# An adaLN transformer block: the last feed-forward's residual and modulation on other engines, another order for the first projections, new planner costs

## The chip, the cores and the metric

The kernel runs on one core of a Trainium2 chip. The metric is the device time of one execution in microseconds (us), lower is better. TensorE (PE) multiplies matrices and transposes, VectorE (DVE) does elementwise work and reductions, ScalarE (ACT) does activations and copies, GpSimd (POOL) does elementwise work that stays in SBUF, and SyncE (SP) issues nearly all DMAs.

## The reference

Two sequences (b = 0, 1) of 2048 tokens with 256 features go through one block:

```
mod = (silu(c) @ wmod)            # six rows of 256 per sequence: sa, ca, ga, sb, cb, gb
ga, gb = sign(.) * max(|.|, 0.25)
h = layernorm(x) * (1 + ca) + sa
q, k, v = h @ wq, h @ wk, h @ wv  # 16 heads, key size 16, value size 64
p = softmax(q k^T / 4, over the queries)      # axis=1: each key normalises over all queries
x = x + ga * ((p @ v) @ wo)
h = layernorm(x) * (1 + cb) + sb
x = x + gb * fp4_linear(silu(fp4_linear(h, w_gate)) * fp4_linear(h, w_up), w_down)
```

`fp4_linear` rounds both operands in blocks of 16 to the grid 0, 0.5, 1, 1.5, 2, 3, 4, 6 times (block maximum / 6). The hidden size is 704. All is float32.

## The kernel before, in words

A planner, not the program's text, sets the order of instructions. Every piece of work is a generator (a *chain*) that yields operations, waits for events and for rooms (buffers), and is added with a due time counted in attention steps. `Order.run` simulates the engines: each operation has a cost from `Queue.estimate` (L285), a dependent one waits for its forerunner (`SAME` on one engine, 0.2 us between engines), and on each engine the operation that can start first goes first, ties by due time. `Free(op)` drops the tie to the chain's previous operation. `Best(first, second, margin)` picks the first engine unless the second would end more than `margin` earlier. The result is a fixed list for each engine; the engines then run their lists strictly in order and wait on semaphores.

The work, in order of time:

- **The start.** The four groups of 512 tokens of x, `wm_a` (sa and ca), wq, wk and `wm_b` (the other modulation rows) are loaded. `mod_columns` (L476) makes silu(c), multiplies it with `wm_a` on TensorE (tile `modt`, 16 small matmuls), and brings the two results out of PSUM on DVE as `sa_t` and `ca1_t`. `norm(0, g)` takes layer-norm statistics on DVE, applies them (`xn`), transposes with TensorE and modulates the transposed tokens (`ht`). `qk(0, 0, i, g)` projects the first eight heads' queries (i = 0) and keys (i = 1) of one group, splits the result into two parts (`st`), and sends it by SP both into the first head's tiles (`q<-st`, two DMAs; `k<-st`, four) and to a DRAM scratch. The first attention step waits for all four query groups and for the first key group. `mod_rows` makes the remaining modulation rows (`modb`, then `mods`).
- **The middle.** 512 attention steps (2 sequences, 16 heads, 16 key tiles): scores on TensorE (`ps`), a pass with a minimum on DVE (`e`), `mn` on POOL, exp on ACT, the reciprocal `rz` on DVE, scaled values `vn` on POOL, and the product with the values on TensorE (`o`). Between the steps lie the projections, the rounding of the weights, and the whole feed-forward of sequence 0.
- **The tail.** Sequence 1's feed-forward has nothing left to hide behind. `project_last` adds the last quad of heads into x (`op` on TensorE, the sum on DVE). `ffn_stats` takes statistics for 1, 3 or 4 tiles of 128 tokens, `tail_norm` applies them (`ffn_apply`: one scale-and-shift, then times `cb` and plus `sb` from `mods`) and rounds with `quantize` (tiles `w`, `am_h`, `s_h`, `r_h`), and `tail(b, t)` does for each of 16 tiles: transpose (`hq`), gate and up projections (`pg`, `pu`), silu and product, `quantize` again (`e`, `am_g`, `s_g`, `r_g`), transpose (`h2t`), down projection (`dn`, weights already times gb), sum with x (`y`) and the store. Tile 15 is cut into two halves (`tail_part`).

`quantize` finds the block maximum `am`, the scale `s = am / 6` with an exact correction (three more small operations), its reciprocal `r`, and then runs five wide passes; the choice between POOL and DVE or ACT and DVE is by margin (`QUANTIZE_MARGIN`, `TAIL_MARGIN`).

Of the kernel before, what the change touches and what calls it, by code (L numbers as in the profile page):

```python
# [32 lines left out]
NPACE = 0.2  # L33
FPACE = 0.4
FFN = 9
MODS_DUE = 3, 4.0
WEIGHTS_DUE = 6, 210
COPY_MARGIN = 0.5
QUANTIZE_MARGIN = 2
WEIGHTS_MARGIN = 3  # L40
TAIL_MARGIN = 1


PROJECT_DUE = -0.5, 1.2, 2, 2
NORM_DUE = -0.4, -0.2, 0.6
STATS_LEAD = 4
NORM_LEAD = 2.5
LAST_LEAD = 0.5
SPLIT = 1
MODS = ("ga", "sb", "cb", "gb")  # L50
# [190 lines left out]
class Queue:  # L241
# [23 lines left out]
    def estimate(self, method, args, kw, emit):  # L265
        out = args[0]
        aps = [a for a in args if isinstance(a, bass.AP)]
        n = max(size(a) for a in aps)
        if method == "dma_start":
            return 0.5, emit, 2.3 + n * out.shape[0] * 4e-6 / 0.35  # L270
        if self.name == "PE":
            if method == "transpose":
                return out.shape[0] / 1200, emit, 0.0, None, "full"

            lhsT, rhs = kw["lhsT"], kw["rhs"]
            passes = 1 if rhs.dtype == F32R else 2
            stream = size(rhs) * passes ** 2 / 2400
            if rhs.shape[0] <= 64:
                first = lhsT.start_partition() == 0
                return (stream + 0.002 if first else 0.005), emit, 0.0, None, "rows"  # L280
            if out.shape[0] <= 64:
                first = out.start_partition() == 0
                return (stream + 0.005 if first else 0.005), emit, 0.0, None, "columns"
            return stream + 0.005, emit, 0.0, None, "full"
        sb = all(a.space != PSUM for a in aps)  # L285
        if self.name == "ACT":
            t = 0.05 + n / 1200 + 0.04 * sb
            func = kw.get("func", args[2] if method == "activation" else None)
            table = {AF.Exp: "exp", AF.Silu: "silu"}.get(func)
            t += 0.093 * sum(isinstance(kw.get(k), bass.AP) for k in ("bias", "scale"))  # L290
            t += 0.17 * isinstance(kw.get("accum_out"), bass.AP)
            return t, emit, 0.0, table
        if self.name == "POOL":
            if method == "tensor_scalar":
                return 0.16 + 0.083 * len(aps[2:]) + n * 0.001, emit
            if n == 1:
                return 0.28, emit
            spread = any(len(a.ap) > 2 and a.ap[-1][0] == 0 for a in aps)
            return 0.08 + n * (0.0019 if spread else 0.0023), emit
        if method == "reciprocal":  # L300
            return 0.07 + n * 0.0063, emit
        scalars = method == "tensor_scalar" and len(aps) > 2
        fast = method in ("tensor_scalar", "tensor_copy") and sb and not scalars
        if fast:
            return 0.065 + n * 0.00052, emit
        if "accum_out" in kw:
            return 0.065 + 0.07 * scalars + n * 0.00104, emit, 0.05
        return 0.03 + 0.035 * (not sb) + 0.06 * (scalars and not sb) + n * 0.00104, emit


@with_exitstack
def adaln_block(
# [85 lines left out]
    def copy(dst, src, margin=None):  # L398
        return either(A.copy(dst, src), V.tensor_copy(dst, src), margin)

    def matmuls(dst, pairs):
        return [
            T.matmul(dst, lhsT=l, rhs=r, start=(k == 0), stop=(k == len(pairs) - 1))
            for k, (l, r) in enumerate(pairs)
        ]

# [65 lines left out]
    nc.gpsimd.memset(magic[:, 0:1], 1.5 * 2.0 ** 22)  # L472
    nc.gpsimd.memset(magic[:, 1:2], -1.5 * 2.0 ** 22)


    def mod_columns():  # L476

        yield Wait(["c"])
        yield A.activation(sig, cs, AF.Exp, scale=-1.0)
        yield V.tensor_scalar(sig, sig, 1.0, None, ALU.add)  # L480
        yield V.reciprocal(sig, sig)
        yield V.tensor_tensor(cs, cs, sig, ALU.mult)
        signal("cs")
        place, _ = yield Wait(["wm_a"], OTHER)
        ps = banks(place, "modt")[:, 0, 0 : 2 * KC * B].rearrange("p (j b) -> p j b", b=B)
        for j in range(2 * KC):
            yield Free(
                matmuls(
                    ps[:, j, :],
                    [(wm_a[:, k, j * P : (j + 1) * P], cs[:, k, :]) for k in range(KC)],  # L490
                )
            )
        give("osb")
        yield V.tensor_copy(sa_t, ps[:, 0:KC, :])
        yield V.tensor_scalar(ca1_t, ps[:, KC :, :], 1.0, None, ALU.add)
        leave(place)
        signal("sa")

# [40 lines left out]
        signal("mods")  # L539


    def ln_stats(x4, name):

        n = x4.shape[1]
        yield Wait(take=["ln"])
# [19 lines left out]
                yield V.scalar_tensor_tensor(r, e, 1.5, r, ALU.add, ALU.mult)  # L565
        yield V.scalar_tensor_tensor(e, e, 0.5, r, ALU.add, ALU.mult)
        yield V.tensor_tensor(r, r, e, ALU.add)
        yield V.scalar_tensor_tensor(c, mv[:, 0:n, 0], -1.0, r, ALU.mult, ALU.mult)
        return c, r

# [13 lines left out]
    SIXTH = 1.0 / 6.0  # L584

    EXPONENT = 0x7F800000

    def blocks(a):
        return a.rearrange("p (n k) -> p n k", k=BLK)
# [20 lines left out]
    def quantize(a, nb, name, m, margin=None):  # L610

        a3 = blocks(a)
        s, r = yield from scales(a3, nb, name)
        yield V.tensor_scalar(r, r, 1.0 - 2.0 ** -23, None, ALU.mult)  # L620
        yield pool(a3, a3, spread(r), ALU.mult, margin=QUANTIZE_MARGIN if margin is None else None)
        yield V.tensor_scalar(m.bitcast(U32), a.bitcast(U32), EXPONENT, None, ALU.bitwise_and)
        yield either(

            [
                A.activation(m, m, AF.Relu, bias=magic[:, 1:2], scale=1.5 * 2.0 ** 22),
                A.activation(m, m, AF.Identity, bias=magic[:, 0:1]),
            ],
            V.tensor_scalar(m, m, 1.0, 1.5 * 2.0 ** 22, ALU.max, ALU.mult),
            margin,  # L630
        )
# [223 lines left out]

    def qk(b, blk, i, n):

        room = "v" if (b, blk, i) == (0, 0, 1) else "st"
        place, _, _ = yield Wait([("ht", b, n), "wk" if i else "wq"], [*OTHER, room])
        if (b, i, blk) not in scratch:  # L860
            scratch[b, i, blk] = dram.tile(
# [290 lines left out]
    def ffn_stats(b, t, n):  # L1152
        yield Wait([("out", b, NQUAD - 1, t + j) for j in range(n)])
        x4 = xs[b, t // 4][:, t % 4 : t % 4 + n, :]
        c, r = yield from ln_stats(x4, f"f{b}_{t}")
        for j in range(n):
            lns[b, t + j] = (c, r, j, n)
        signal(("ln", b, t))

    def ffn_apply(h, b, t, margin=None):  # L1160
        c, r, j, n = lns[b, t]
        yield ln_apply(h, x_tile(b, t), j, c, r, margin)
        if signal(("applied", b, t - j), of=n):
            give("ln")
        for which, op in (("cb", ALU.mult), ("sb", ALU.add)):
            args = h, h, mod(b, which), op
            op = G.tensor_tensor(*args)
            yield op if margin is None else Best(op, V.tensor_tensor(*args), margin=margin)

    def finish(ps, y, place, b, t):  # L1170
        yield V.tensor_tensor(y, ps[:, 0:D], mod(b, "gb"), ALU.mult)
# [79 lines left out]
            )  # L1251
        signal("wdb")

    def down(ps, h2t, wd):
        return matmuls(ps[:, 0:D], down_pairs(h2t, wd))
# [17 lines left out]
    def tail(b, t):  # L1273
# [46 lines left out]
        yield from transpose_hidden(e, h2t, f"h2t{b}_{t}", TAIL_MARGIN)  # L1320
        yield Wait(["wdb"], ["o"])
        ps = ps_o.tile([P, 512], F32, tag="o", name=f"dn{b}_{t}")
        for c, op in enumerate(down(ps, h2t, tails["w"])):
            yield Free(op) if c else op
        give("e")
        yield from tail_out(b, t, ps)

    def tail_out(b, t, ps):
        yield Wait(take=["h"])
        y = w2.tile([P, D], F32, tag="h", name=f"y{b}_{t}")  # L1330
        yield V.tensor_tensor(y, ps[:, 0:D], x_tile(b, t), ALU.add)
        give("o")
        yield S.dma_start(out[b, t * P : (t + 1) * P, :], y)
        give("h")
# [1 line left out]
    def tail_part(b, t, i, e, pg, pu, places):  # L1336
# [17 lines left out]
        if i == 0:  # L1354
            yield Wait(["wdb"], ["o"])
            tails["o", b, t] = ps_o.tile([P, 512], F32, tag="o", name=f"dn{b}_{t}")
        else:
            yield Wait([("down", b, t)])
        ps = tails["o", b, t]
        for c, r in enumerate(CHUNK[3 * i : 3 * i + 3]):  # L1360
# [4 lines left out]
                start=(i == 0 and c == 0),  # L1365
                stop=(i == 1 and c == 2),
            )
        signal(("down", b, t))
# [126 lines left out]
```

## Time and profile before

| | |
|---|---|
| median of 3 runs | 2009.36 us (2007.64 to 2009.44) |
| profiled execution: its own time | 2009.48 us |
| its span, first to last instruction | 2007.4 us |
| busy: PE, DVE, ACT, POOL | 1913.4, 1728.3, 1328.1, 696.5 us |
| first score matmul, last attention matmul ends | 46.95 us, about 1806.1 us |
| the tail after that | about 201 us |

A line of the timeline gives: start, duration, engine, line of kernel.py, operation, output<-inputs, shapes, count, and in brackets how long the engine stood idle before it and what released it. Nearly every operation has line L251, because one helper records them all; tile names tell them apart. The rows of windows give, for each stretch, its length and the busy time of PE, its weight loads (PEld), DVE, ACT and POOL, with the number of instructions, then the granted TensorE clock as a share, the DMA share and the GB/s moved.

### The profile page before, as it was taken

How to read it: one execution, taken by the hardware profiler on the slowest of the kernel's cores; microseconds unless marked ns; L12 is line 12 of the kernel's file. 1: busy time of each engine (PE TensorE's matmuls, PEld its weight loads, DVE VectorE, ACT ScalarE, POOL GpSimd, SP SyncE). 2: the span in 40 equal slices, each digit the busy share in tenths (PEclk: the TensorE clock that was granted, in tenths of full speed). 3: DMA queues.
4: the chain of work that ended last, by engine and by line, in shares of the span. 5: the costliest groups of instructions: out<-in, count | busy, mean ns of one | idle time of the engine just before them, and what ended most of it. 6: DMA issues, size and time to landing. Idle time of an engine off the chain costs nothing. (4 is left out here: it accounts for less than half of the span.)

```text
span 2007.4 us, 30123 instructions
## 1 busy us (share of the span) xinstructions
PE 1913.4 (95%) x10084; PEld 773.7 (39%) x10084; DVE 1728.3 (86%) x4102; ACT 1328.1 (66%) x1412; POOL 696.5 (35%) x1449
## 2 busy tenths in 40 slices
PE   6999999999999989999999999999999999998887
PEld 3433333333333323343333434344443333335555
DVE  5899889988999988879988788887889778988786
ACT  3577767766777666776777667775677767782341
POOL 0323333333343331112444344444533112233553
PEclk9999999999999999999999999999999999999999
DMA  7212121112111123211112211111011111100000
GB/s 215 75 53 58 47 58 48 38 32 48 33 44 33 38 63 90 74 38 48 28 31 58 61 32 40 40 37 36 4 38 40 33 32 32 32 1 0 16 12 16
DMA packets 40394, 88.00 MB, mean 44 GB/s; under 512 B 6320, under 2 KB 22576, under 8 KB 36272
## 3 DMA queue, kind: packets, MB, share of 16 engines
q1 hardware_dynamic: 38880, 83.98, 16.3%
q10 hardware_dynamic: 1360, 2.10, 0.3%
q8 instruction: 81, 1.33, 0.3%
q14 instruction: 73, 0.60, 0.1%
HBM read 63.51 MB, written 20.97 MB: 42 GB/s over the span
## 5 line engine op out<-in xcount | busy, mean ns | idle before, releaser
L251 DVE TENSOR_SCALAR_CACHE_REDUCE e<-ps 128x1024 f32<-128x1024 f32 x1024 | 1221.5, 1218 | 132.6 <-PE ps L251 83.0
L251 ACT ACTIVATE e<-e,mn 128x2048 f32<-128x2048 f32 x512 | 1025.1, 2002 | 454.5 <-POOL mn L251 453.0
L251 PE MATMUL o<-e,vn 128*64 128x512 f32 x4096 | 994.4, 603 | 25.2 <-POOL vn L251 20.5
L251 PEld LDWEIGHTS o<-e,vn 128*64 128x64 f32 x4096 | 253.4, 136 | 483.9 <-issue 352.9
L251 POOL TENSOR_SCALAR mn<-mn 128x1 f32<-128x1 f32 x512 | 155.4, 304 | 804.6 <-DVE rz L251 358.8
L251 PE MATMUL ps<-q,k 64*128 64x512 f32 x2048 | 383.6, 448 | 10.4 <-DVE e L251 6.2
L251 PEld LDWEIGHTS ps<-q,k 64*128 64x128 f32 x2048 | 157.0, 184 | 377.4 <-DVE rz L251 108.9
L251 POOL TENSOR_SCALAR vn<-v,rz 128x64 f32<-128x64 f32 x512 | 168.2, 329 | 327.1 <-DVE rz L251 262.9
L251 PE MATMUL v<-wv,ht 128*64 128x256 f32 x1024 | 124.6, 386 | 0.8 <-ACT v L251 0.4
L251 PE MATMUL op<-wo,osb 128*64 128x256 f32 (+1 forms) x960 | 123.3, 381 | 1.2 <-ACT hqt L251 0.8
L251 DVE RECIPROCAL rz<-z 128x1 f32<-128x1 f32 x512 | 80.6, 157 | 24.5 <-ACT e L251 23.0
L251 PEld LDWEIGHTS op<-wo,osb 128*64 128x64 f32 (+1 forms) x960 | 76.0, 140 | 59.1 <-issue 29.7
L251 ACT ACTIVATION_READ_ACCUMULATOR e<-e,mn 128x1 f32 x512 | 95.5, 186 | 0.0
L251 PEld LDWEIGHTS v<-wv,ht 128*64 128x64 f32 x1024 | 71.4, 138 | 59.3 <-issue 25.4
L251 DVE DVE_READ_ACCUMULATOR e<-ps 128x1 f32 x1024 | 84.9, 83 | 0.0
L251 ACT COPY osb<-o 64x512 f32<-64x512 f32 x102 | 59.1, 580 | 13.1 <-PE o L251 10.5
L251 PE MATMUL qk<-ht,wqk_sb 128*64 128x512 f32 (+1 forms) x224 | 65.0, 606 | 1.1 <-ACT ht L251 0.9
L251 POOL TENSOR_TENSOR h<-h,m 128x704 f32<-128x704 f32 x32 | 54.1, 1691 | 10.7 <-ACT m L251 5.9
L251 PE MATMUL dn<-wdb,e 117*128 117x256 f32 (+1 forms) x192 | 49.0, 406 | 9.1 <-ACT e L251 9.1
L251 DVE TENSOR_TENSOR x<-op,x 128x1024 f32<-128x1024 f32 (+2 forms) x37 | 39.8, 1075 | 15.6 <-PE op L251 15.4
L251 PE MATMUL pg<-wg_t,w 128*128 128x352 f32 x128 | 47.8, 517 | 4.2 <-ACT w L251 4.1
L251 PE MATMUL dn<-wd_t,h2t 117*64 117x256 f32 (+1 forms) x384 | 47.0, 383 | 0.0
(239 smaller groups left out, 1499.6 us busy)
## 6 DMA issues: line engine op xcount, KB each, us to landing
k<-scr SPq DMA_DIRECT2D x124, 256.0 KB, 4.7
scr<-st SPq DMA_DIRECT2D x32, 512.0 KB, 3.1
q<-scr SPq DMA_DIRECT2D x124, 128.0 KB, 5.7
x<-in_x_dram SPq DMA_DIRECT2D x8, 512.0 KB, 4.2
wv<-in_wv_dram SPq DMA_DIRECT2D x8, 256.0 KB, 5.5
wo<-in_wo_dram SPq DMA_DIRECT2D x8, 256.0 KB, 4.1
xt<-in_x_dram SPq DMA_DIRECT2D x4, 512.0 KB, 7.0
out_dram<-h2t SPq DMA_DIRECT2D x16, 128.0 KB, 1.7
```

The costliest lines, as they stand in the source:

```text
L251: op = Op(self.name, *self.estimate(method, args, kw, lambda: f(*args, **kw)))
```

## The change

- **Start.** 64 transposes of the identity are put on TensorE before anything else, and 16 more behind `sa`; their results are never read. `sa_t` and `ca1_t` are made by ACT. The projections of the keys of groups 1 to 3 are moved from before the attention to its steps (due 0.5, 4.5, 8.5), and `mod_rows` from due 3 and 4 to 5 and 6.
- **Planner.** The cost of a DVE operation on SBUF changes from 0.03 to 0.067 us plus its elements, and a `scalar_tensor_tensor` with a per-partition operand costs 0.05 us more.
- **quantize** (both sequences). The reciprocal is taken of the maximum and not of the scale, so the exact scale is made beside the first wide pass. The number of small DVE operations stays 7. In the tail the pass that makes `m` has a margin of 2.0 for ACT.
- **Tail.** The modulation becomes two DVE operations: (x - mean) * cb, then * r + sb. The residual is a matmul of the identity with x that opens the PSUM accumulation of `dn`; the result is copied out by ACT or DVE. `TAIL_MARGIN` goes from 1 to 0.5, `NORM_LEAD` from 2.5 to 3.5, and the due times of the last output projections from -0.5, 1.2, 2, 2 to -0.5, 0.0, 0.2, 0.4.

```diff
-MODS_DUE = 3, 4.0
+MODS_DUE = 5, 6.0
+BUSY = 64, 16
-TAIL_MARGIN = 1
+TAIL_MARGIN = 0.5
+MAGIC_MARGIN = 2.0
-PROJECT_DUE = -0.5, 1.2, 2, 2
+PROJECT_DUE = -0.5, 0.0, 0.2, 0.4
-NORM_LEAD = 2.5
+NORM_LEAD = 3.5
...
-        return 0.03 + 0.035 * (not sb) + 0.06 * (scalars and not sb) + n * 0.00104, emit
+        pointer = 0.05 if method == "scalar_tensor_tensor" and len(aps) > 3 else 0.0
+        return 0.067 + pointer + 0.06 * (scalars and not sb) + n * 0.00104, emit
...
+    def busy(n, after):
+        place, _ = yield Wait(after, OTHER)
+        ps = banks(place, f"busy{n}")
+        for _ in range(n):
+            yield Free(T.transpose(ps[:, 0, 0:P], ident, ident))
+        leave(place)
...
-        yield V.tensor_copy(sa_t, ps[:, 0:KC, :])
-        yield V.tensor_scalar(ca1_t, ps[:, KC :, :], 1.0, None, ALU.add)
+        yield A.copy(sa_t, ps[:, 0:KC, :])
+        yield Free(A.activation(ca1_t, ps[:, KC :, :], AF.Identity, bias=1.0))
...
     def quantize(a, nb, name, m, margin=None):
-        s, r = yield from scales(a3, nb, name)
-        yield V.tensor_scalar(r, r, 1.0 - 2.0 ** -23, None, ALU.mult)
+        yield V.tensor_reduce(am, a3, AX.X, ALU.max, apply_absolute_value=True)
+        yield V.tensor_scalar(am, am, SMALLEST, None, ALU.max)
+        yield V.reciprocal(r, am)
+        yield Free(V.tensor_scalar(s, am, SIXTH, None, ALU.mult))
+        yield V.tensor_scalar(r, r, 6.0 - 3 * 2.0 ** -21, None, ALU.mult)
+        yield V.scalar_tensor_tensor(q, s, -4.0, am, ALU.mult, ALU.add)
         yield pool(a3, a3, spread(r), ALU.mult, margin=QUANTIZE_MARGIN if margin is None else None)
+        yield Free(V.scalar_tensor_tensor(q, s, -2.0, q, ALU.mult, ALU.add))
         yield V.tensor_scalar(m.bitcast(U32), a.bitcast(U32), EXPONENT, None, ALU.bitwise_and)
+        yield Free(V.scalar_tensor_tensor(s, q, SIXTH, s, ALU.mult, ALU.add))
...
-            margin,
+            margin if margin is None else MAGIC_MARGIN,
...
-        room = "v" if (b, blk, i) == (0, 0, 1) else "st"
+        room = "v" if (b, blk) == (0, 0) and (i == 1 or n % 2) else "st"
...
+    def residual(ps, b, t):
+        return T.matmul(ps[:, 0:D], lhsT=ident, rhs=x_tile(b, t), start=True, stop=False)
...
     def tail_norm(b, t, n):
-            yield from ffn_apply(w[:, 0, j, :], b, t + j, margin)
+            yield Free(
+                V.scalar_tensor_tensor(
+                    h, x, mean[:, k : k + 1], mod(b, "cb"), ALU.subtract, ALU.mult
+                )
+            )
...
+            yield Free(
+                V.scalar_tensor_tensor(h, h, r[:, k : k + 1], mod(b, "sb"), ALU.mult, ALU.add)
+            )
...
-        for c, op in enumerate(down(ps, h2t, tails["w"])):
-            yield Free(op) if c else op
+        yield Free(residual(ps, b, t))
+        for op in down(ps, h2t, tails["w"], first=False):
+            yield Free(op)
...
     def tail_out(b, t, ps):
-        yield V.tensor_tensor(y, ps[:, 0:D], x_tile(b, t), ALU.add)
+        yield copy(y, ps[:, 0:D], TAIL_MARGIN)
...
+    add(busy(BUSY[0], []), -70)
     add(mod_columns(), -60)
+    add(busy(BUSY[1], ["sa"]), -51)
     for g in range(NG):
         add(norm(0, g), -50 + 3 * g)
-        for i in range(2):
-            add(qk(0, 0, i, g), -49 + 3 * g + i)
+        add(qk(0, 0, 0, g), -49 + 3 * g)
+        add(qk(0, 0, 1, g), -48 if g == 0 else 4 * g - 3.5)
```

More of the change, by code (lines that the diff above doesn't have):

```diff
@@ L399, in copy, with matmuls @@
         return either(A.copy(dst, src), V.tensor_copy(dst, src), margin)
-    def matmuls(dst, pairs):
+    def matmuls(dst, pairs, first=True):
         return [
-            T.matmul(dst, lhsT=l, rhs=r, start=(k == 0), stop=(k == len(pairs) - 1))
+            T.matmul(dst, lhsT=l, rhs=r, start=(first and k == 0), stop=(k == len(pairs) - 1))
             for k, (l, r) in enumerate(pairs)
@@ L483, in mod_columns @@
         signal("cs")
+        due(-60)
         place, _ = yield Wait(["wm_a"], OTHER)
@@ L539, in mod_rows, with ln_stats @@
         signal("mods")
-    def ln_stats(x4, name):
+    def ln_stats(x4, name, centre=False):
         n = x4.shape[1]
@@ L567, in ln_stats @@
         yield V.tensor_tensor(r, r, e, ALU.add)
+        if centre:
+            return mv[:, :, 0], r
         yield V.scalar_tensor_tensor(c, mv[:, 0:n, 0], -1.0, r, ALU.mult, ALU.mult)
@@ L586, in adaln_block @@
     EXPONENT = 0x7F800000
+    SMALLEST = 5.999999976025183e-12
     def blocks(a):
@@ L618, in quantize @@
         a3 = blocks(a)
-        s, r = yield from scales(a3, nb, name)
-        yield V.tensor_scalar(r, r, 1.0 - 2.0 ** -23, None, ALU.mult)
+        yield Wait(take=["qs"])
+        am = small.tile([P, nb], F32, tag="am", name=f"am_{name}", bufs=3)
+        s = small.tile([P, nb], F32, tag="qs", name=f"s_{name}", bufs=3)
+        r = small.tile([P, nb], F32, tag="qr", name=f"r_{name}", bufs=3)
+        q = small.tile([P, nb], F32, tag="qq", name=f"q_{name}", bufs=2)
+        yield V.tensor_reduce(am, a3, AX.X, ALU.max, apply_absolute_value=True)
[4 more added lines that the diff above has]
+        yield V.scalar_tensor_tensor(q, s, -4.0, am, ALU.mult, ALU.add)
         yield pool(a3, a3, spread(r), ALU.mult, margin=QUANTIZE_MARGIN if margin is None else None)
+        yield Free(V.scalar_tensor_tensor(q, s, -2.0, q, ALU.mult, ALU.add))
         yield V.tensor_scalar(m.bitcast(U32), a.bitcast(U32), EXPONENT, None, ALU.bitwise_and)
+        yield Free(V.scalar_tensor_tensor(s, q, SIXTH, s, ALU.mult, ALU.add))
         yield either(
@@ L1154, in ffn_stats @@
         x4 = xs[b, t // 4][:, t % 4 : t % 4 + n, :]
-        c, r = yield from ln_stats(x4, f"f{b}_{t}")
+        c, r = yield from ln_stats(x4, f"f{b}_{t}", centre=b == B - 1)
         for j in range(n):
@@ L1158, in ffn_stats, with ffn_apply @@
         signal(("ln", b, t))
-    def ffn_apply(h, b, t, margin=None):
+    def ffn_apply(h, b, t):
         c, r, j, n = lns[b, t]
-        yield ln_apply(h, x_tile(b, t), j, c, r, margin)
+        yield ln_apply(h, x_tile(b, t), j, c, r)
         if signal(("applied", b, t - j), of=n):
@@ L1165, in ffn_apply @@
         for which, op in (("cb", ALU.mult), ("sb", ALU.add)):
-            args = h, h, mod(b, which), op
-            op = G.tensor_tensor(*args)
-            yield op if margin is None else Best(op, V.tensor_tensor(*args), margin=margin)
+            yield G.tensor_tensor(h, h, mod(b, which), op)
     def finish(ps, y, place, b, t):
@@ L1252, in weight_tail, with down @@
         signal("wdb")
-    def down(ps, h2t, wd):
-        return matmuls(ps[:, 0:D], down_pairs(h2t, wd))
+    def down(ps, h2t, wd, first=True):
+        return matmuls(ps[:, 0:D], down_pairs(h2t, wd), first)
     def down_pairs(h2t, wd):
         return [(h2t[0:n, c, :], wd[0:n, c, :]) for c, n in enumerate(CHUNK)]
+    def residual(ps, b, t):
+        return T.matmul(ps[:, 0:D], lhsT=ident, rhs=x_tile(b, t), start=True, stop=False)
     def tail_norm(b, t, n):
@@ L1265, in tail_norm @@
         for j in range(n):
-            yield from ffn_apply(w[:, 0, j, :], b, t + j, margin)
+            mean, r, k, of = lns[b, t + j]
+            h, x = w[:, 0, j, :], x_tile(b, t + j)
+            yield Free(
[3 more added lines that the diff above has]
+            )
+            signal(("centred", b, t + j))
+        for j in range(n):
+            mean, r, k, of = lns[b, t + j]
+            h = w[:, 0, j, :]
+            yield Wait([("centred", b, t + j)])
+            yield Free(
+                V.scalar_tensor_tensor(h, h, r[:, k : k + 1], mod(b, "sb"), ALU.mult, ALU.add)
+            )
+            if signal(("applied", b, t + j - k), of=of):
+                give("ln")
         h, m = (w[:, i, 0:n].rearrange("p j d -> p (j d)") for i in range(2))
@@ L1356, in tail_part @@
             tails["o", b, t] = ps_o.tile([P, 512], F32, tag="o", name=f"dn{b}_{t}")
+            yield Free(residual(tails["o", b, t], b, t))
         else:
@@ L1364, in tail_part @@
                 rhs=tails["w"][0:r, 3 * i + c, :],
-                start=(i == 0 and c == 0),
+                start=False,
                 stop=(i == 1 and c == 2),
```

## The prediction, made before the changed kernel ran

> **What bounds the kernel now.** I read the page first, then the windows by stage, then the timelines of the start and of the tail, and last the waits of TensorE.
>
> ```profile
> PE 1913.4 (95%) x10084; PEld 773.7 (39%) x10084; DVE 1728.3 (86%) x4102; ACT 1328.1 (66%) x1412; POOL 696.5 (35%) x1449
> PE   6999999999999989999999999999999999998887
> ```
>
> TensorE is the bound on average. The first slice and the last four show where it is not full. The windows (length; busy PE, PEld, DVE, ACT, POOL; granted clock; DMA) put numbers on it:
>
> ```profile
> 10.00:15.00 5.00, 2.84 (x14) 2.75 (x13) 2.17 (x21) 0.00 (x0) 0.00 (x0) 1.00 1.05 377
> 40.00:60.00 20.00, 16.10 (x73) 7.90 (x73) 15.05 (x42) 6.04 (x8) 1.23 (x3) 0.91 0.79 206
> 600.00:800.00 200.00, 187.18 (x996) 68.63 (x994) 181.19 (x454) 136.84 (x146) 61.44 (x143) 1.00 0.22 56
> 1860.00:1880.00 20.00, 14.99 (x52) 10.26 (x51) 12.70 (x40) 3.63 (x6) 11.27 (x8) 0.83 0.04 14
> ```
>
> Adding the windows, TensorE is idle 18.2 us of the first 60, 39 us of the 1740 between 60 and 1800, and 37 us of the last 207. The clock is below full in the tail, so part of its busy time there is slow work. Three stages, three limits, and the change touches all three.
>
> In the start, TensorE waits and then runs slowly:
>
> ```profile
> 9.27 3.57 PE L251 MATMUL modt<-cs,wm_a 128*128 128x2 f32 x16 [9.27 <-DVE cs L251]
> 12.88 0.16 DVE L251 COPY sa_t<-modt 128x4 f32<-128x4 f32 x1 [2.80 <-PE modt L251]
> 15.64 2.07 ACT L251 ACTIVATE xn<-x,ln3a,ln1a 128x256 f32<-128x256 f32 x4 [10.53 <-DVE ln3a L251]
> 19.33 3.78 PE L251 MATMUL qk<-ht,wqk_sb 128*128 128x512 f32 x4 [0.87 <-ACT ht L251]
> 25.83 1.88 PE L251 MATMUL qk<-ht,wqk_sb 128*128 128x512 f32 x4
> 51.40 0.47 PE L251 MATMUL ps<-q,k 64*128 64x512 f32 x1 [2.68 <-DMA q<-st]
> ```
>
> DVE stands 2.80 us before `sa_t`, with the layer-norm chain queued behind it, so `xn` starts only at 15.64. The same four projections take 3.78 us at 19.33 and 1.88 at 25.83: the first run at half clock. (The granted clock reads 1.00 there; the durations decide.) The second half of the scores waits at 51.40 for the last query group.
>
> **The start, step by step.** (1) 64 transposes begin when the identity is ready, at about 1.4 us. Eight slow ones took 1.91 us (`ht` at 22.90, 0.24 each), eight fast ones 1.04 (at 30.98, 0.13 each). The tail's restarts show how long a slow stretch lasts: 5.2 to 6.3 us. So about 23 are slow (5.5 us) and 41 fast (5.3 us): the end is near 12.2. `modt`, ready at 9.27, starts then, and takes 16 x 0.13 = 2.1 us instead of 3.57: end 14.3 instead of 12.84. This step alone loses 1.5 us. (2) The two copies on ACT cost 2 x 0.2 (its small ACTIVATE took 0.20): `sa` at 14.7. The layer-norm chain is no longer behind it on DVE and is done by then, so `xn` starts at 14.8 and not 15.64, the transposes end about 17.0 and not 18.46 (the 16 more transposes, 2.1 us, end before the second `xn` does), and `qk` starts at about 17.8: 1.5 us earlier. (3) At full clock: `qk` 3.78 - 1.88 = 1.9; the eight `ht` transposes 0.9; the first two `modb` 1.38 - 0.94 = 0.4; the 32 `v` matmuls at 51.8, after the wait for the queries, 5.36 - 3.67 = 1.7. Sum 4.9. (4) Queries first: of PE's 27 us of work between 19.3 and 47, three key groups (3 x 1.72) and most of `modb` now follow the queries, and on SP three times four `k<-st` (2.5 us of issue) and a scratch store (0.6) no longer stand before `q<-st`. The idle pieces between 47 and 51.8 (3.5 us) go. What is late next is PE itself: the moved 12 us are done among the steps. SP has the head loads there (4.6 us of issue between 55 and 61, for step 16), with room for 9. Together 1.5 + 4.9 + 3.5 = 9.9. Below is zero, were the moved work to push the steps out by as much. I take 7.
>
> Here a rule speaks against the change. The row: the clock rose near 25.3 us, after 6 us of PE work of which 1.9 were transposes. The Trainium skill, "TensorE: Matmul & The Clock Gate", Part 4 (PE-mode transpose), says that the full clock does not engage for transposes, since they do not count as busy. By that rule all 64 stay slow: 1.4 + 64 x 0.24 = 16.8, `modt` slow to 20.4, `xn` at 20.8, 5 us late, and the 4.9 us of step 3 mostly gone: the start would win 9.9 - 6.5 - 4.9, about -1.5, a loss. By the row it wins. In the 3.4 us before the rise only some 1.9 were matmuls, while 3.4 us of matmuls from 19.33 on had not raised it; I follow the row.
>
> **The middle.** Work is unchanged (7 small DVE operations per `quantize`, before and after). Only the order changes, through the planner's DVE cost. Two independent operations show what is right:
>
> ```profile
> 1816.09 0.42 DVE L251 TENSOR_TENSOR w<-w,r_h 128x256 f32<-128x256 f32 x1
> 1816.43 0.15 DVE L251 SCALAR_TENSOR_TENSOR ln2f<-ln2f,ln1f 128x3 f32<-128x3 f32 x1
> ```
>
> The next starts 0.34 after a 256-wide one. The old cost gives 0.03 + 0.266 = 0.296, the new 0.333. So the planner's DVE was too fast by some 0.04 on each SBUF operation, and its lists run late on DVE. But a dependent operation starts 0.46 after (1812.73 to 1813.18), which the old cost plus 0.16 met exactly; the new says 0.49. The waits of PE between 60 and 1804 that this order can move:
>
> ```profile
> PE o L251 <- POOL vn L251: 20.3, 32, 1.5
> PE ps L251 <- DVE e L251: 6.2, 10, 1.3
> ```
>
> No row prices a reordering. Bounds: 13 us gained if a third of the 39 goes, 25 lost if these waits double. I take a gain of 2.
>
> **The tail.** The rows of groups and waits from 1804 on:
>
> ```profile
> L251 POOL TENSOR_TENSOR w<-w,mods 128x256 f32<-128x256 f32 x28 | 22.3, 813 | 22.4 <-ACT w L251 22.0
> L251 DVE TENSOR_TENSOR y<-dn,x 128x256 f32<-128x256 f32 x16 | 6.7, 421 | 16.4 <-PE dn L251 16.4
> PE dn L251 <- ACT e L251: 9.1, 11, 0.9
> PE hq L251 <- POOL w L251: 9.0, 4, 4.9
> PE h2t L251 <- POOL e L251: 5.5, 5, 3.0
> 1820.03 4.66 PE L251 MATMUL pg<-wg_t,w 128*128 128x352 f32 x8 [0.46 <-ACT w L251]
> ```
>
> Removed: POOL's 22.3 us, ACT's 15 scale-and-shifts (8.4), DVE's 16 sums (6.7) and 5 modulation operations (2.6). Added on DVE: 32 operations of 256 with a per-partition operand; the nearest row occupies 0.34, the planner adds 0.05: 32 x 0.38 = 12.2. Added on ACT: 16 copies at 0.37 (`w<-hq`), 6.0, and the `m` passes that leave DVE (7 at 0.52 there, 0.88 on ACT, 6.2). DVE also waits for POOL: a small `s_g` takes 0.17 alone and 1.54 at 1972.45 beside a POOL operation. The groups of `s_g`, `r_g`, `s_h` and `r_h` have means of 0.27 to 0.39 against 0.17 to 0.19 alone, and with the wide passes I count some 20 us of such excess; a quarter of POOL's 89 us leaves, so 5. DVE net: -6.7 - 2.6 + 12.2 - 3.6 - 5 = -5.7.
>
> Added on PE: 16 residuals, two passes of 0.217 (`dn` 2.60 / 12): 6.9 us. They need neither `h2t` nor ACT, so they fit into the 0.9 us that PE stands before `dn` in 11 cases of 16. Visible: 5 x 0.43 = 2.2. If that cover were gone it would be 6.9.
>
> Beginning of the tail: PE is idle from 1813.25 to 1818.91 (5.65 us), then runs `pg` slowly (4.66 against 2.37 later), while 5.2 us of `op` lie on the chain at 1827 and 1836. The new due times put these into the gap, which also keeps the clock up: up to 5.2 + 2.3 = 7.5. But four more sums of 0.68 on DVE fall into the first tile's chain, against 1.4 us that shorter statistics, two modulation steps and an earlier reciprocal save. I take 5. The rest: of the 14.5 us that PE waits for POOL's results, with DVE nearly 6 us lighter, I take a third, 5, less 2.2 for residuals. In the last tile two ACT passes replace a DVE one (+0.7 per half) and the scale chain is 0.6 shorter: nothing. The tail gains 8, between 0 and 15.
>
> **Sum.** 7 + 2 + 8 = 17 off the profiled execution's 2009.5 (span 2007.4 and 2.1 around it), which stands 0.1 above the median: 1992.
>
> **The rivals.**
> - *The middle gives it back (slower).* With dearer DVE the margins send more wide passes to POOL, where `mn` and `vn` of every step stand in line behind them (0.6 to 1.7 us each). For it: `vn` already ends 20.3 of PE's waits. Against: POOL is 35% busy. It decides once these waits grow by more than 15 us; doubled, with `ps` behind them, they cost 20 to 25: about 2014.
> - *The clock stays low in the start*, by the rule above: the start loses 1.5 instead of gaining 7, 2001.
> - *One end is hidden.* The start's gain comes back as waits between 100 and 800 us, where DVE is 92% busy, or the tail's DVE, already full in its first 20 us, eats its gain. Then 7 to 10 remain: 2002.
>
> **Chances.** The forecast 0.60 (own range 1978 to 2000), one end hidden 0.17, clock low 0.10, middle gives it back 0.13. About 0.2%, or 4 us, is what a measurement of this kernel can tell from no change. Faster: 0.60 and most of the second and third, 0.80. Same: 0.08. Slower: 0.12. The range, 1976 to 2006, leaves out the slower rival and the gains beyond both bounds.
>
> **What would show it.** `modt` starts at 12 us at 2 us for 16, the first `qk` near 18 takes 1.9, the first full scores near 40. In the tail POOL's `w<-w,mods` is gone, PE has no gap of 5 us between `op` and `hq`, and `dn` has 14 instructions a tile. I am wrong if `modt` ends near 20, if `vn` ends more than 30 us of PE's waits, or if the tail after the last `o` is not under 197 us.

## The result: 1 per cent faster, and the profile after

The changed kernel takes 1988.5 us (median of 4, 1986.46 to 1988.77) against 2009.07 for the kernel before (median of 4): ratio 0.9897, 95% interval 0.9880 to 0.9914. That is 20.6 us less where 17 had been forecast. Its profiled execution took 1986.46 with a span of 1984.7, so its profile shows 22.7 us less span; some 2 us of that are this execution's luck: it is the fastest of the four, with a granted clock of 0.996 where the others have 0.993 and 0.994.

The start of every exp (512 of them, one a step) gives the split. Against the profile of before, the changed kernel is ahead by 7.9 us at the third step (number 2), by 4.5 at step 64, 4.6 at 192, 11.2 at 224 and 9.1 at the last one. The remaining 13.6 us come after it. So: start 4, middle 5, tail 13.6, where the prediction had 7, 2 and 8. The sum was nearly right by luck: all three terms were not.

The page of after and two windows (same columns as before):

```profile
PE 1919.7 (97%) x10196; PEld 782.1 (39%) x10196; DVE 1714.8 (86%) x4125; ACT 1341.3 (68%) x1438; POOL 622.0 (31%) x1387
PE   8999999999999989999999999999999999998988
...
600.00:800.00 200.00, 191.20 (x1014) 70.27 (x1012) 183.45 (x460) 137.74 (x149) 60.75 (x144) 1.00 0.22 58
1860.00:1880.00 20.00, 18.75 (x85) 13.72 (x84) 19.32 (x59) 9.59 (x16) 3.51 (x3) 1.00 0.04 14
```

The stretch from 1860 to 1880 shows the tail's change in one line: POOL 3.5 us instead of 11.3, VectorE full at 19.3, TensorE 18.75 instead of 15, the clock at 1.00 instead of 0.83.

The start, in the timeline of after:

```profile
1.37 9.32 PE L253 MATMUL busy<-ident 128*128 128x128 f32 x64 [1.37 <-POOL ident masks.py:199]
10.53 1.84 PE L253 MATMUL modt<-cs,wm_a 128*128 128x2 f32 x16
12.41 0.16 ACT L253 COPY sa_t<-modt 128x4 f32<-128x4 f32 x1 [7.22 <-PE modt L253]
13.20 2.08 ACT L253 ACTIVATE xn<-x,ln3a,ln1a 128x256 f32<-128x256 f32 x4 [0.55 <-DVE ln3a L253]
16.69 1.99 PE L253 MATMUL qk<-ht,wqk_sb 128*128 128x512 f32 x4 [0.93 <-ACT ht L253]
46.20 0.50 PE L253 MATMUL ps<-q,k 64*128 64x512 f32 x1 [1.83 <-DMA q<-st]
```

Up to the first `qk` the prediction's start is there, a little earlier than worked out: the 64 transposes end at 10.7 and not 12.2, and `modt` and the first `qk` run at full clock. The first full scores are late: they were to come near 40 and came at 46.20, 5.2 us earlier than before, for TensorE still waits 1.83 us there for `q<-st`. And `xn` waits for `ln3a`, VectorE's chain, and not for `sa`. That matters below.

The clock during the transposes, 1 us a line:

```profile
4.00:5.00 1.00, 1.00 (x6) 1.00 (x6) 0.17 (x1) 0.99 (x2) 0.00 (x0) 1.00 1.09 382
5.00:6.00 1.00, 1.00 (x8) 1.00 (x7) 0.93 (x5) 0.19 (x1) 0.00 (x0) 1.00 1.00 329
6.00:7.00 1.00, 1.00 (x11) 1.00 (x10) 0.31 (x2) 0.00 (x0) 0.00 (x0) 1.00 1.06 383
```

Before 5.75 us a transpose starts every 0.213 us, after it every 0.109 (a row also counts those that reach over its edges), and nothing but transposes has run on TensorE. (The record of the granted clock begins at 5.75; the distance between starts decides.)

The tail, waits of TensorE after the last attention matmul, and the groups of POOL and of two VectorE operations there:

```profile
PE pg L253 <- ACT w L253: 6.4, 10, 1.5
PE hq L253 <- DVE x L253: 5.2, 1, 5.2
PE h2t L253 <- DVE e L253: 3.5, 2, 3.0
PE dn L253 <- ACT e L253: 2.5, 5, 0.6
PE op L253 <- DVE x L253: 2.1, 1, 2.1
...
L253 POOL TENSOR_TENSOR w<-w,s_h 128x512 f32<-128x512 f32 x7 | 8.5, 1212 | 99.8 <-DVE w L253 95.6 <-DVE q_g L253 4.2
L253 POOL TENSOR_TENSOR e<-e,s_g 128x704 f32<-128x704 f32 x3 | 4.2, 1387 | 38.5 <-DVE q_h L253 28.8 <-DVE e L253 9.6
L253 POOL TENSOR_TENSOR e<-e 128x704 f32<-128x704 f32 x1 | 1.7, 1687 | 14.4 <-DVE e L253 14.4
...
L253 DVE TENSOR_TENSOR e<-e,r_g 128x704 f32<-128x704 f32 x15 | 13.2, 877 | 0.0
L253 DVE TENSOR_SCALAR r_g<-r_g 128x44 f32<-128x44 f32 x15 | 2.6, 176 | 0.0
```

POOL's wide passes have all but gone, not only the 28 of the modulation: 15 `e<-e` became 1, 15 `e<-e,s_g` became 3, and POOL is busy for 14 us of the tail instead of 89. No wait of TensorE names POOL any more. Beside the emptied POOL a small `r_g` takes 176 ns; in the tail of before it took 344 on average. The groups there:

```profile
L251 POOL TENSOR_TENSOR e<-e 128x704 f32<-128x704 f32 x15 | 25.2, 1683 | 47.4 <-DVE e L251 19.1 <-DVE r_g L251 13.8 <-DVE s_h L251 10.7
L251 POOL TENSOR_TENSOR e<-e,s_g 128x704 f32<-128x704 f32 x15 | 23.4, 1561 | 1.0
...
L251 DVE TENSOR_SCALAR r_g<-r_g 128x44 f32<-128x44 f32 x15 | 5.2, 344 | 0.1
```

But one gap has stayed: the first transpose (`hq`) waits 5.2 us for `x`, at 1816.88, 19.8 us after the last attention matmul. Before, it came after 12.8.

The waits are not all. Here is the whole tail as one window, of before, of after and of a run that comes below (a3):

```profile
1806.15:2007.41 201.26, 164.56 (x640) 115.71 (x640) 161.24 (x453) 64.52 (x100) 88.73 (x73) 0.93 0.03 11
1797.05:1984.68 187.63, 163.72 (x672) 118.06 (x672) 161.36 (x485) 75.85 (x120) 14.33 (x11) 0.96 0.03 12
1805.87:2019.67 213.80, 174.29 (x640) 122.44 (x640) 160.53 (x455) 63.51 (x98) 88.80 (x73) 0.88 0.03 10
```

TensorE's waits in the tail fell by 12.7 us (33.4 to 20.7). Its busy time stayed, although 6.9 us of residuals came in, with less of it slow: TensorE was at half clock for 27.3 us of the tail before and for 13.7 after. The two belong together. In all 14 traces, after its first change, the clock changes only at steps of 3.41 us. Each of the 61 steps at full clock in which TensorE stood idle for more than 1.9 us was followed by a step at half clock, and none of the 7870 in which it stood idle for less than 1.3 (of the 59 between, 13 were). So a long wait is paid twice: as idle time, and by up to 1.7 us of lost work in the next step.

### The profile page after: what moved, and what is told of

Read it like the earlier page. It is cut to its first block, busy times and chain, and to the rows that moved or that the text cites. A ratio compares the mean times of both kernels' runs of the same rounds, so it can differ in the third digit from the quotient of the medians.

```text
span 1984.7 us, 30266 instructions
## 1 busy us (share of the span) xinstructions
PE 1919.7 (97%) x10196; PEld 782.1 (39%) x10196; DVE 1714.8 (86%) x4125; ACT 1341.3 (68%) x1438; POOL 622.0 (31%) x1387
## 5 line engine op out<-in xcount | busy, mean ns | idle before, releaser
L253 ACT COPY osb<-o 64x512 f32<-64x512 f32 x101 | 58.4, 579 | 18.6 <-PE o L253 17.2
L253 DVE TENSOR_TENSOR x<-op,x 128x1024 f32<-128x1024 f32 (+2 forms) x37 | 39.7, 1074 | 15.9 <-PE op L253 15.6
L253 PE MATMUL pg<-wg_t,w 128*128 128x352 f32 x128 | 46.7, 507 | 6.4 <-ACT w L253 6.4
```

Of the source, the lines that this page charges most:

```text
L253: op = Op(self.name, *self.estimate(method, args, kw, lambda: f(*args, **kw)))
```

## The experiments

All medians and ratios are against the kernel before on the same chip (2008.46, 2008.62 and 2007.93 in the three groups). "Last step" is how far the last exp is ahead of the profile of before; the last four columns are from each kernel's profile, after the last attention matmul, and "clock" is the mean granted clock of TensorE.

| kernel | median us | ratio, 95% interval | last step | tail us | waits of PE in it | POOL busy in it | clock in it |
|---|---|---|---|---|---|---|---|
| before | 2009.07 | 1 | 0 | 201.3 | 33.4 | 88.7 | 0.93 |
| changed | 1988.50 | 0.9897, 0.9880 to 0.9914 | 9.1 | 187.6 | 20.7 | 14.3 | 0.96 |
| a1, start only | 2005.16 | 0.9981, 0.9974 to 0.9989 | 3.9 | 201.4 | 33.8 | 88.2 | 0.93 |
| a2, planner cost only | 2010.97 | 1.0019, 1.0010 to 1.0028 | 7.0 | 215.8 | 42.0 | 89.2 | 0.89 |
| a3, rounding order only | 2021.48 | 1.0061, 1.0046 to 1.0076 | 0.3 | 213.8 | 36.0 | 88.8 | 0.88 |
| a4, tail only | 1992.06 | 0.9917, 0.9902 to 0.9932 | 0.9 | 184.0 | 17.4 | 15.5 | 0.97 |
| b1, changed, old margin | 2001.56 | 0.9964, 0.9951 to 0.9977 | 9.1 | 203.5 | 28.4 | 69.3 | 0.93 |
| c1, before, new margin | 1999.39 | 0.9955, 0.9940 to 0.9970 | -0.3 | 191.3 | 25.5 | 42.3 | 0.94 |
| b7, changed, old modulation | 1991.36 | 0.9915, 0.9898 to 0.9931 | 8.7 | 191.7 | 21.6 | 43.1 | 0.95 |
| b2, changed, old due times of op | 1983.78 | 0.9879, 0.9864 to 0.9893 | 6.5 | 184.5 | 18.6 | 18.3 | 0.96 |
| b3, changed, residual by VectorE | 1981.46 | 0.9863, 0.9847 to 0.9880 | 7.2 | 181.4 | 22.8 | 19.2 | 0.98 |
| b6, changed, old rounding order | 1980.63 | 0.9860, 0.9845 to 0.9875 | 9.0 | 182.3 | 15.6 | 24.4 | 0.97 |
| b4, changed, no idle transposes | 1983.97 | 0.9879, 0.9865 to 0.9894 | 9.1 | 184.8 | 19.4 | 14.4 | 0.96 |
| c2, b2, b3 and b6 together | 1991.35 | 0.9915, 0.9898 to 0.9931 | 10.0 | 192.8 | 30.1 | 21.2 | 0.94 |

How far such numbers carry: b4 and the changed kernel have the same lists of instructions on all engines after the start, yet their tails took 184.8 and 187.6 us in the two profiles, and their ratios differ by 0.0018 with overlapping intervals. Kernels with the same list in the middle (changed, b1, b2, b3, b4) reach the last step 6.5 to 9.1 ahead; that spread is already there at step 2 (6.1 to 8.1), where b2 and b3, the two that are behind, have two half-clock steps near 46 us, changed and b1 one, and b4 none. So 3 us between two rows are nothing, and since b4 has the changed kernel's tail, what is taken out of the changed kernel is compared with both below.

### One stage at a time

The start alone:

```diff
 # before, with
-MODS_DUE = 3, 4.0
+MODS_DUE = 5, 6.0
...
-        yield V.tensor_copy(sa_t, ps[:, 0:KC, :])
+        yield A.copy(sa_t, ps[:, 0:KC, :])
...
+    add(busy(BUSY[0], []), -70)
...
+    add(busy(BUSY[1], ["sa"]), -51)
...
+        add(qk(0, 0, 1, g), -48 if g == 0 else 4 * g - 3.5)
```

> The kernel before with only the start changed (64 and 16 transposes of the identity, modulation's columns by ScalarE, key projections of groups 1 to 3 and the modulation's rows later). Theory 'three stages that add up' (the two traces put the changed kernel 7.9 us ahead at the second attention step, 4 from step 12 to 144, 9.1 at the last step, and 22.7 at the end): about 4 us faster, near 2005; ahead by 7 to 8 at the second step, by 4 at step 16, and no more than that at the last step. Rival 'the start is given back': the steps between 60 and 110 us are held by VectorE whatever the start does, and the gain is below 2 us, 2007 to 2009. Rival 'the start carries the middle': the shifted start is what also gives the 5 us in the middle: 9 us faster, 2000.

2005.16 us. Its first full scores come at 41.40, 10.0 us earlier than before. It is ahead by 14.0 us at step 2, where 7 to 8 were expected, then by 7.3 at step 8, 4.9 at 16, 3.7 at 64, and 3.9 at the end. The first theory's end value holds. The steps are not held by the start in the middle: from 64 on the lead is constant to 0.3 us. The work that was moved there (three key projections of 1.7 us and the modulation's rows) is of the size to shrink it between steps 2 and 64; no run shows that by itself.

The planner's VectorE cost alone:

```diff
-        return 0.03 + 0.035 * (not sb) + 0.06 * (scalars and not sb) + n * 0.00104, emit
+        pointer = 0.05 if method == "scalar_tensor_tensor" and len(aps) > 3 else 0.0
+        return 0.067 + pointer + 0.06 * (scalars and not sb) + n * 0.00104, emit
```

> The kernel before with only the planner's VectorE cost changed (0.03 to 0.067 us on SBUF, 0.05 more with a per-partition operand). Theory 'three stages': the cost is what gains 5 us in the middle (between steps 176 and 240 in the trace), so 3 to 6 us faster there; in the tail dearer VectorE operations send more to GpSimd, so nothing or a loss of up to 3: in all 2004 to 2007. Rival 'order by luck': any other list of instructions moves the middle by a few us either way, and this one alone is within 2 us of the kernel before.

2010.97 us, slower. The middle is what the theory said: between 2.8 behind and 1.3 ahead until step 192, then 5.0 us ahead at 256 and 7.0 at the end. Whether any other list would have gained as much, as the rival has it, was not tried. The tail lost more than the theory allowed: 14.5 us in the profiled execution, which was 6 us above its own median (granted clock 0.986, against 0.990 near the median), so some 9 in a usual one. TensorE's waits there, in words of the trace:

```profile
PE h2t L251 <- POOL e L251: 16.0, 5, 8.4
PE dn L251 <- ACT e L251: 10.0, 10, 1.6
```

The first was 5.5 us before. With the same 15 passes of each kind on POOL, other neighbours in the lists made TensorE wait for them up to 8.4 us at a time. Its waits grew by 8.6 us in all, and its busy time by 5.2 for the same 640 matmuls, with the clock at 0.89.

The rounding order alone (reciprocal of the maximum, the scale beside the first wide pass):

```diff
-        s, r = yield from scales(a3, nb, name)
-        yield V.tensor_scalar(r, r, 1.0 - 2.0 ** -23, None, ALU.mult)
+        yield V.tensor_reduce(am, a3, AX.X, ALU.max, apply_absolute_value=True)
+        yield V.tensor_scalar(am, am, SMALLEST, None, ALU.max)
+        yield V.reciprocal(r, am)
+        yield Free(V.tensor_scalar(s, am, SIXTH, None, ALU.mult))
+        yield V.tensor_scalar(r, r, 6.0 - 3 * 2.0 ** -21, None, ALU.mult)
...
```

> The kernel before with only the new order in the rounding (reciprocal of the maximum, the exact scale beside the first wide pass). Theory 'three stages': the work is the same, the chain to the first wide pass is three operations of about 0.2 us shorter; in the middle nothing, in the tail two chains a tile, of which VectorE's queue hides most: 0 to 4 us faster, 2005 to 2009. Rival 'the shorter chain makes the tail': 8 us or more.

2021.48 us: both theories fail. The middle stays (0.3 us), the tail gets 12.5 us longer, with POOL as busy as before. TensorE waits 11.2 us for POOL's `e` instead of 5.5, but in sum only 2.6 us more. The larger part is its busy time: 9.7 us more for the same 640 matmuls (164.56 and 174.29 in the windows above), with 15 half-clock steps in the tail instead of 8. A shorter chain and the same work made the tail slower mainly by the clock; which operation of the new order makes the waits fall so was not tried.

The tail alone (residual, modulation, margins, leads, due times; not the rounding, not the planner's cost), the changed kernel less all else:

```diff
 # the changed kernel, with
-MODS_DUE = 5, 6.0
+MODS_DUE = 3, 4.0
...
-    add(busy(BUSY[0], []), -70)
-    add(busy(BUSY[1], ["sa"]), -51)
...
-        pointer = 0.05 if method == "scalar_tensor_tensor" and len(aps) > 3 else 0.0
+        return 0.03 + 0.035 * (not sb) + 0.06 * (scalars and not sb) + n * 0.00104, emit
...
-        yield V.reciprocal(r, am)
+        s, r = yield from scales(a3, nb, name)
```

> The kernel before with the tail changed (residual by TensorE, modulation in two VectorE operations, the margins, the leads and the due times of the last projections), without the new start, the new planner cost and the new rounding. Theory 'three stages': 10 to 13 us faster, 1996 to 1999, all of it after the last attention step, with GpSimd's wide passes of the tail mostly gone. Rival 'the parts need each other': with the old, lower VectorE costs the margins choose otherwise and without the shorter rounding chain less than 6 us is left.

1992.06 us, 16 faster where 10 to 13 were expected, and the rival fails. The tail is 17.3 us shorter, more than in the changed kernel (13.6). So the four parts alone give, by their ratios, -3.8, +3.8, +12.3 and -16.7: a sum of -4.4 us where the whole gives -20.6. They don't add. The planner's cost and the rounding order lengthen the tail of before by 14.5 and 12.5 us in their profiles (a2, a3), and hurt little in a tail from which POOL's passes are gone: the changed kernel's has both and is only 3.6 us longer than a4's.

### Which number of the tail did it

`TAIL_MARGIN` says by how many us earlier VectorE must end, by the planner's reckoning, before POOL loses a pass to it.

```diff
 # b1: the changed kernel, with
-TAIL_MARGIN = 0.5
+TAIL_MARGIN = 1
```

> The changed kernel (1988.5, its tail 192.4 us after the last exp, GpSimd's wide passes there 17 us against 92 before) with TAIL_MARGIN back at 1. Theory 'the margin empties GpSimd': the passes on e (15 of each kind at 1.7 and 1.6 us before) go back to GpSimd, the waits of TensorE for GpSimd's e return (5 to 16 us in the runs that had them), and the tail is 5 to 10 us longer: 1993 to 1998. Rival 'the modulation empties it': taking the 28 modulation passes off GpSimd is what matters, and the margin moves the time by less than 2 us.

2001.56 us, 13 slower than the changed kernel (17 than b4), more than the 5 to 10 expected: all 15 passes of each kind go back to POOL, as its groups and TensorE's waits in the tail show:

```profile
L253 POOL TENSOR_TENSOR e<-e 128x704 f32<-128x704 f32 x15 | 28.1, 1873 | 77.2 <-DVE e L253 37.8 <-DVE r_h L253 14.7 <-PE dn L253 7.3
L253 POOL TENSOR_TENSOR e<-e,s_g 128x704 f32<-128x704 f32 x15 | 23.7, 1580 | 1.1
...
PE h2t L253 <- POOL e L253: 12.5, 4, 4.5
```

(two groups of POOL and one wait of TensorE, both after the last attention matmul of b1) and the wait for them returns. POOL was not short of time: it stood idle for 77 us before these passes, mostly waiting for VectorE. It is slow at them (1.6 to 1.9 us against 0.88 on VectorE), and two of them stand one behind the other in each tile's chain to `h2t`. Beside them VectorE's small `r_g` takes 316 ns again instead of 176; this run does not separate that from the length of the passes. The clock is at 0.93 again. The tail is 203.5 us, no better than before the change, although modulation, residual and leads are the new ones.

The same number alone, in the kernel before:

```diff
 # c1: the kernel before, with
-TAIL_MARGIN = 1
+TAIL_MARGIN = 0.5
```

> The kernel before with one number changed, TAIL_MARGIN from 1 to 0.5. Undoing this number in the changed kernel cost 13 us, as much as the whole tail had gained. Theory 'GpSimd's wide passes are the tail's brake, whatever else is done': 6 to 12 us faster, 1997 to 2003, GpSimd's passes on e down from 30 to 10 or fewer, TensorE's waits for GpSimd's e gone. Rival 'the margin works only with the modulation off GpSimd': its 28 modulation passes (22 us) keep the queue full, and the time is within 3 us of 2009.

1999.39 us, 8.5 faster by one number, as the first theory said: POOL's 30 passes on `e` fall to 6, no wait for POOL is left in TensorE's list, and that with the 28 modulation passes still on POOL (groups of POOL in the tail of c1):

```profile
L251 POOL TENSOR_TENSOR w<-w,mods 128x256 f32<-128x256 f32 x28 | 25.4, 922 | 50.4 <-ACT w L251 49.9
L251 POOL TENSOR_TENSOR e<-e 128x704 f32<-128x704 f32 x3 | 5.0, 1677 | 12.1 <-DVE r_g L251 8.5 <-DVE s_h L251 3.6
...
L251 POOL TENSOR_TENSOR e<-e,s_g 128x704 f32<-128x704 f32 x3 | 4.2, 1386 | 41.9 <-DVE r_g L251 28.9 <-DVE e L251 13.1
```

From the other side, the old modulation in the changed kernel:

```diff
 # b7: the changed kernel, with
-                V.scalar_tensor_tensor(
-                    h, x, mean[:, k : k + 1], mod(b, "cb"), ALU.subtract, ALU.mult
-                )
...
+            yield from ffn_apply(w[:, 0, j, :], b, t + j, margin)
```

> The changed kernel with the old modulation (scale-and-shift on ScalarE or VectorE, then two passes on GpSimd or VectorE by the margin of 0.5). Theory 'VectorE and ScalarE carry too much in the tail; GpSimd had room': the 28 passes go back to GpSimd in part, VectorE loses about 12 us of work[...]: within 3 us of the changed kernel, 1985 to 1992. Rival 'a busy GpSimd brakes whatever it does': 5 us or more slower, above 1993.

1991.36 us, with POOL busy for 43 us in the tail. That is 3 us above the changed kernel, as the first theory said, but 7 above b4, whose interval its own does not meet. So the modulation in two VectorE operations is worth 3 to 7 us, less than the margin, and the rival is not excluded.

### The parts that were to cost little

Due times of the last projections:

```diff
-PROJECT_DUE = -0.5, 0.0, 0.2, 0.4
+PROJECT_DUE = -0.5, 1.2, 2, 2
```

> The changed kernel with the old due times of the last output projections (-0.5, 1.2, 2, 2). In the changed kernel the first transpose of the tail starts 19.8 us after the last attention matmul, against 12.8 before: the four more sums on VectorE stand in the first tile's chain. Theory 'the early projections cost more than they hide': the first transpose is 4 to 6 us earlier, 24 matmuls of op (5.2 us) return to the full part of the tail, of which VectorE's rhythm hides some: 1 to 4 us faster, 1985 to 1987. Rival 'TensorE is what is full': every one of the 5.2 us counts and the gap is merely moved: same or up to 2 us slower, 1988 to 1991.

1983.78 us. The first transpose is 7.3 us earlier (12.5 after the last attention matmul instead of 19.8), and the rest of the tail 4.2 longer (172.0 instead of 167.8). The difference, 3.1 us, points the way of the first theory, but b4 with the changed kernel's own tail has the same ratio: not settled. It does show that the early projections did not shorten the tail.

The residual back on VectorE:

```diff
-        yield Free(residual(ps, b, t))
-        for op in down(ps, h2t, tails["w"], first=False):
-            yield Free(op)
+        for c, op in enumerate(down(ps, h2t, tails["w"])):
+            yield Free(op) if c else op
...
-        yield copy(y, ps[:, 0:D], TAIL_MARGIN)
+        yield V.tensor_tensor(y, ps[:, 0:D], x_tile(b, t), ALU.add)
...
```

> The changed kernel with the residual added by VectorE again (16 sums from PSUM at 0.42 us), no identity matmul, no copy by ScalarE. Theory 'VectorE is the tail's bound': 6.7 us return to an engine that is 94% busy in the tail from 1860 on, 6.9 us leave TensorE, which has room for them: 3 to 6 us slower, 1991 to 1995. Rival 'TensorE is the bound': 2 to 5 us faster, 1984 to 1986.

1981.46 us, 7 faster than the changed kernel, with intervals that only touch, and 3 faster than b4. The rival has the direction right; the size lies between 3 and 7 us. TensorE's waits in the tail without the residual:

```profile
PE dn L253 <- ACT e L253: 9.8, 11, 1.1
PE hq L253 <- DVE x L253: 5.2, 1, 5.2
PE pg L253 <- ACT w L253: 3.3, 9, 0.5
```

The residual did go into the wait before `dn`: 9.8 us without it, 2.5 with it. But elsewhere TensorE waits more with it: 6.4 instead of 3.3 for ACT's `w` (ACT has 16 more copies, `y`), 3.5 instead of 0.4 for VectorE's `e`. In sum the waits are only 2.1 us less for 6.9 us more work.

The old rounding order:

```diff
-        yield V.tensor_reduce(am, a3, AX.X, ALU.max, apply_absolute_value=True)
-        yield V.tensor_scalar(am, am, SMALLEST, None, ALU.max)
-        yield V.reciprocal(r, am)
...
+        s, r = yield from scales(a3, nb, name)
+        yield V.tensor_scalar(r, r, 1.0 - 2.0 ** -23, None, ALU.mult)
...
```

> The changed kernel with the old order in the rounding (scale first, then its reciprocal), the margin of the magic pass kept. Alone, the new order made the tail of the kernel before 12.6 us longer and left the middle as it was. Theory 'it hurts through GpSimd only': with GpSimd nearly empty in the tail, the shorter chain is worth what it saves, 0 to 3 us: 1988 to 1992 here. Rival 'it hurts in any company': the old order is 3 us or more faster, 1980 to 1985.

1980.63 us, 8 faster than the changed kernel and 4 faster than b4; the rival holds. The waits of TensorE are the fewest of all (15.6 us). So the new order costs some 4 to 8 us also where POOL is nearly empty, little above what such numbers carry. Which of its operations does it was not tried; both orders have 7 small operations and the chain to the first wide pass is shorter in the new one.

The idle transposes taken out:

```diff
-    add(busy(BUSY[0], []), -70)
...
-    add(busy(BUSY[1], ["sa"]), -51)
```

> The changed kernel without the 80 transposes of the identity. Theory 'they raise the clock': modt is at half clock again (16 in 3.6 us) but starts at 9.4 instead of 10.5, the first qk takes 3.8 instead of 2.0, the second attention step is 3 to 4 us later; of that 1 to 2 us are left at the last step, since the start alone also kept only 3.9 of its first 14: 1989 to 1991. Rival 'they only warm': no difference at the last step, within 0.7 us of 1988.5.

Ahead by 8.1 us at step 2 and 9.1 at the last step: the same as with them, as the rival had it. The timeline of the start without the transposes:

```profile
9.40 3.57 PE L253 MATMUL modt<-cs,wm_a 128*128 128x2 f32 x16 [9.40 <-DVE cs L253]
13.13 2.07 ACT L253 ACTIVATE xn<-x,ln3a,ln1a 128x256 f32<-128x256 f32 x4
16.87 3.78 PE L253 MATMUL qk<-ht,wqk_sb 128*128 128x512 f32 x4 [0.93 <-ACT ht L253]
46.84 0.50 PE L253 MATMUL ps<-q,k 64*128 64x512 f32 x1 [1.83 <-DMA q<-st]
```

`modt` and `qk` are slow again, yet `xn` starts 0.07 us earlier, for `modt` starts at 9.40, before the transposes would have ended; and the 1.8 us that `qk` loses shrink to 0.6 by the first full scores, where TensorE waits for a DMA in both. The half-clock step that the changed kernel has at 46.7 us is absent here, and by step 2 that gain is gone too. The median, 1983.97, is 4.5 us below the changed kernel's, where the rival had allowed 0.7. What is left to have made the start faster is the rest of a1's edit: the engine of `sa_t` and `ca1_t`, the order of the queries, and the later projections; these were not run one by one.

All three that were faster undone, together (b2, b3 and b6 in one):

```diff
-PROJECT_DUE = -0.5, 0.0, 0.2, 0.4
+PROJECT_DUE = -0.5, 1.2, 2, 2
...
+        s, r = yield from scales(a3, nb, name)
...
-        yield copy(y, ps[:, 0:D], TAIL_MARGIN)
+        yield V.tensor_tensor(y, ps[:, 0:D], x_tile(b, t), ALU.add)
```

> The changed kernel with the three parts undone that were faster undone: the early due times of the last projections, the residual by TensorE, the new rounding order. Theory 'their costs add': 4.7, 7.0 and 7.9 us one by one, with overlap (all three relieve the same tail) some 10 to 16 us faster than the changed kernel, 1972 to 1979. Rival 'each only reshuffles the list': no faster than the best single one, 1980 to 1984.

1991.35 us: they don't add, and the three together are slower than each, which neither theory had. TensorE waits 30.1 us in this tail, 11.5 of it for VectorE before three `hq`, and its clock is at 0.94, where b3 has 22.8 us and 0.98. The best versions are b6 and b3, 0.9860 and 0.9863: both are 27 to 28 us faster than before, 7 to 8 than the changed kernel, and 3 to 4 than b4.

## Why the prediction was right, and where its steps were wrong

- *The total*: 17 forecast, 20.6 measured, because three wrong terms nearly cancelled; that was luck. The likeliest case was the right one as to sign and size, not as to cause.
- *Start, 7 forecast, 3.9 measured* (a1; 4.6 in the changed kernel at step 192). Steps 1 and 2 were right in kind (`xn` at 13.20 where 14.8 was worked out; 20 slow transposes at 0.21 us and 44 fast ones at 0.11, where 23 at 0.24 and 41 at 0.13 were assumed). Up to the first full scores a1 gains 10.0 us, as the 9.9 of the sum had it; the changed kernel gains only 5.2 there, for a wait of 1.83 us for `q<-st` stays. The mis-sized terms are the 4.9 us "at full clock", worth nothing at the last step (b4), and "what is late next is PE itself": 10 of a1's first 14 us are gone by step 64, where I had taken off 2.9 of 9.9. That was the rival "one end is hidden", in part.
- *The rule against the transposes*, in the Trainium skill, "TensorE: Matmul & The Clock Gate", Part 4 (PE-mode transpose): the clock rose 4.4 us after the first transpose (3.0 to 5.2 us in the eight traces that have them) with nothing else on TensorE, so following the row was right, and the measurement decides against the rule for these float32 transposes. But I made 11 us hang on it (9.9 against -1.5), and at the last step it was worth nothing (b4).
- *Middle, 2 forecast, 5 measured* (9.1 less the start's 3.9; 7.0 alone in a2). The reading of the two operations 0.34 us apart, that the planner's VectorE was too fast, was right. The gain lies between steps 192 and 224, where the transposes and the first query and key projections of sequence 1 are done; TensorE's wait for `e` before `ps` between 60 us and the tail fell from 6.2 to 2.1, that for `vn` from 20.3 to 18.6. The slower rival's mechanism, more passes on POOL and longer waits for `vn`, did not appear: POOL's busy time in the middle is as it was.
- *Tail, 8 forecast, 13.6 measured.* Four steps failed. First, its beginning: 5 gained was forecast, but the first transpose came 7 us later; "four more sums of 0.68 on DVE fall into the first tile's chain" was seen and under-priced, and PE's gap of 5 us that I said would go is still there. Second, POOL: only the 22.3 us of modulation were taken off it, so the effect of `TAIL_MARGIN`, a number that I listed and never priced, was missing. It sends 26 more wide passes to VectorE, and it is the largest single cause of the whole change: 13 us undone (b1), 8.5 alone (c1). Third, the residual's cover: at `dn` it was better than "visible 2.2" (the wait is 9.8 us without the residual and 2.5 with it), but other waits grew and the whole costs 3 to 7 (b3). Fourth, the clock: I read that part of TensorE's busy time in the tail was slow work and priced only 2.3 us of it, at the beginning. The half-clock time fell by 13.6 us, and in a3 the clock did most of the harm.
- *DVE net -5.7*: VectorE's busy time in the tail did not move (161.2 and 161.4 us). It took over POOL's passes, and what the small operations of the rounding took too long beside POOL paid for much of that: 182 of them took 52.8 us before and 37.2 after, a gain of 15.6 where 5 were assumed.

Open: which operation of the new rounding order brings the longer waits (a3, b6), and why b2, b3 and b6 together are slower than each. In a2, a3 and c2 the slower tail has more waits and a lower clock at once, so a small shift in the list is enlarged; what the shift is needs its own runs.

## What to carry to other kernels

An engine with spare time can still be the brake: POOL was 44% busy in this tail, and two of its passes in each tile's chain of dependent steps cost time, by their length, by slowing VectorE beside them, or both. Price every number in a diff, also the small ones that choose between engines; one margin was worth 8 to 13 of the 21 us here. Read the granted clock next to the waits: a tail that grows without more waiting may be running slowly. And where an order comes from a list scheduler, take parts out of the new version as well as putting them into the old one: the parts here add up to 4 us, the whole gives 21.

## What the runs showed of the hardware

- Transposes alone raised TensorE's clock: one every 0.213 us from 1.37 us on, one every 0.109 after 5.75 us.
- TensorE's clock fell to half for one to three steps of 3.41 us at a time. In the 14 traces it fell after each of the 61 full-clock steps with more than 1.9 us of idle time and after none of the 7870 with less than 1.3. The tail of before had eight such steps, that of the changed kernel four, that of a3 fifteen.
- A VectorE operation on 44 elements in each partition (`r_g`) took 176 ns with POOL nearly idle, and 316 on average in b1, which differs from that kernel in one margin and has 33 more wide passes on POOL (26 of them on `e`); another of that size (`s_g`) took up to 1.54 us in the kernel before.
